# A two-way decaying scan with a binary-weight product: where ScalarE's short instructions stand, and the last batch's product turned round

## The chip, the core and the metric

The kernel runs on one core of one Trainium2 chip. Its engines work side by side and meet at semaphores: PE (TensorE, matrix products; PEld is its loading of weights), DVE (VectorE), ACT (ScalarE), POOL (GpSimd) and SP (SyncE, which here only issues DMAs). Each engine takes its instructions in the order in which the program gives them. The metric is device time in microseconds (us), lower is better.

## The reference, cut to what matters

Four batches of 1024 tokens with 1024 channels. `kv` serves as both k and v, `x` as the gate r and as the residual.

```python
tf    = sigmoid(sum(time_emb, -1))                              # one number per batch
decay = exp(-exp(w)) * (0.5 + 0.5 * tf)                         # per batch and channel
ek, ekv = exp(min(k, 30)), exp(min(k, 30)) * k
num, den = scan(ekv), scan(ek)         # forward plus backward, a = a * decay + term
num  += exp(min(u + k, 30)) * k - ekv
den  += exp(min(u + k, 30))     - ek
y     = sigmoid(x) * num / max(den, 1e-8) * (0.8 + 0.2 * tf)
alpha = mean(abs(weight), axis=1)                               # per output channel
out   = x + y @ (where(weight >= 0, 1, -1) * alpha[:, None]).T + bias
```

## The kernel before

**The blocks.** The main loop has 32 blocks `g` = 4 batches x 8 groups of 128 channels (`b, cc = divmod(g, NC)`). In a block 128 channels lie on the partitions and the 1024 tokens along the free axis, so that a scan over tokens is one DVE instruction. Everything is written out by hand under `tc.manual_schedule()`: an engine's order is the order of the statements in the loop (L456 to L541).

**DVE** does, in block g: the forward scan of num (L305), the own terms (L295), the backward scan of num (L318), the forward scan of den (L305), the newton-and-gate step of block g-1 (L357), the backward scan of den (L318), the numerator terms of block g+1 (L289), and at the head of the next block the denominator's own term (L327). A backward scan starts from a column `init`, which ACT makes from the last column of the forward scan: `act_edge` (L307), called edge_num and edge_den.

**POOL** does: the DMA that adds the own term into num (L323), the adds of x (L150, below), the floor of den of block g-1 (L333), the clamp of block g (L285), two low parts of block g-2 (L370), the product of den with the reciprocal (L350), that of num (L353) and the gated product (L360). The two low parts stand apart: one ahead of L350, one behind L353.

**ACT** does: the high parts of block g-2 (`act_hi`, L365), the scaling of product groups out of PSUM (`act_scale`, L393), Ln (`act_log`, L340), edge_num, the reciprocal as an exponential (L345), copies of turned groups to SBUF (`act_leave`, L410), the exponentials of block g+1 (L275, L281), edge_den, and in every odd block the sigmoids of the gates of blocks g+1 and g+2 (L111). A sigmoid needs another table than Ln and Exp: one table load before the sigmoids and one after (L94). From batch 1 on the first of the two sigmoids stands ahead of edge_den and the second behind it.

**The product.** gated = hi + lo, two float32r halves of a float32. A group `q` is a batch, a half of the tokens (h, 512) and 128 output channels (oc): 48 groups in batches 0 to 2, 16 in the last. `pe_product` (L375) keeps the weight's signs stationary and moves 512 tokens, 16 matmuls into one PSUM bank; the result has output channels on the partitions. So `act_scale` can scale by alpha and add the bias per partition; four transposes (`pe_turn`, L398) bring tokens back to the partitions, `act_leave` copies the group to a staging tile, and a pair of groups is stored from the SP queue. Then x is added in DRAM by a DMA that accumulates (`add_x`, L147, 128 token rows at a time, from POOL's queue). Batches 0 to 2 run nine blocks behind their scans (`lag`): two groups in most blocks, three in blocks 27, 29 and 31 (`jobs`, L420), so that all 48 are started by the end of the loop. Which block issues which add is set at L429: blocks 15 to 31 without 19 and 27, two in some, and six behind the loop.

**The tail** (L544 on) finishes block 31 and does the last batch's 16 groups. x is loaded as residual tiles (`load_residual`), up to five groups are accumulated ahead over the channel groups that are ready, the rest of block 31 is worked out (floor, den's product and the gated product on DVE; num's product on POOL), and then for each group: product, scale, four transposes, DVE's addition to the residual tile (L405), store.

Of the kernel before, what the change touches and what calls it, by code (L numbers as in the profile page):

```python
# [21 lines left out]
def kernel(  # L22
# [91 lines left out]
    def group(q):  # L114
        b, r = divmod(q, NH * NC)
        h, oc = divmod(r, NC)
        return b, h, oc


    def pair_of(t, q):  # L120
        b, h, oc = group(q)
        return t[b, h * H : (h + 1) * H, oc * P : (oc + 2) * P].rearrange(
            "(n p) c -> p n c", p=P
        )

    def hold(q, t):
        x_pairs[q] = t
        x_res[q], x_res[q + 1] = t[:, :, :P], t[:, :, P:]
# [5 lines left out]
    def load_residual(q, pool, tag):  # L134
        t = pool.tile([P, PER, 2 * P], F32, tag=tag, name=f"x_res_{q}")
        nc.sync.dma_start(out=t, in_=pair_of(x, q))
        hold(q, t)

    def store(q):
        nc.sync.dma_start(out=pair_of(out, q), in_=x_pairs[q])  # L140

    def store_one(q):
        b, h, oc = group(q)
        rows = out[b, h * H : (h + 1) * H, oc * P : (oc + 1) * P]
        nc.sync.dma_start(out=rows.rearrange("(n p) c -> p n c", p=P), in_=x_res[q])
# [34 lines left out]
    decay_ps = ps_c.tile([P, B, NC], F32, tag="decay_ps", name="decay_ps")  # L180
# [123 lines left out]
    def forward(g, t):  # L304
        nc.vector.tensor_tensor_scan(t, decay_row(g), t, 0.0, ALU.mult, ALU.add)  # L305
# [19 lines left out]
    def dve_denominator(g):  # L325
        b, cc = divmod(g, NC)
        nc.vector.scalar_tensor_tensor(  # L327
            dens[g], eus[g], top[:, b, cc : cc + 1], dens[g], ALU.min, ALU.add
        )

    def floor_den(g, engine=nc.gpsimd):
        b, cc = divmod(g, NC)
        engine.tensor_scalar(  # L333
            dens[g], dens[g], F32_MAX, floor[:, b, cc : cc + 1], ALU.min, ALU.max
        )


    def act_log(g):
        b, cc = divmod(g, NC)
        nc.scalar.activation(eus[g], dens[g], AF.Ln, scale=gain[:, b, cc : cc + 1])  # L340

    def act_reciprocal(g):
        b, cc = divmod(g, NC)
        rec = eus[g]
        nc.scalar.activation(  # L345
            rec, rec, AF.Exp, scale=-1.0, bias=ln_g[:, b, cc : cc + 1]
        )

    def den_product(g, engine=nc.gpsimd):
        engine.tensor_mul(dens[g], dens[g], eus[g])  # L350

    def pool_num_product(g):
        nc.gpsimd.tensor_mul(nums[g], nums[g], eus[g])  # L353

    def dve_newton_gate(g):
        den = dens[g]
        nc.vector.scalar_tensor_tensor(den, den, -2.0, sg_ps[g], ALU.add, ALU.mult)  # L357

    def gated_product(g, engine=nc.gpsimd):
        engine.tensor_mul(nums[g], dens[g], nums[g])  # L360
# [7 lines left out]
    def lo_part(g, h, engine=nc.gpsimd):  # L368
        t = gated[divmod(g, NC) + (h,)]
        engine.tensor_sub(  # L370
            t[:, 1, :], nums[g][:, h * H : (h + 1) * H], t[:, 0, :].bitcast(F32)
        )
# [31 lines left out]
    def dve_residual(q):  # L404
        nc.vector.tensor_add(x_res[q], x_res[q], turned[q])  # L405
# [13 lines left out]

    jobs = {g: [] for g in range(steps)}  # L420
    q = 0
    for g in range(lag, steps):
        n = 2 if g <= (B - 1) * NC + 1 or g % 2 == 1 else 3
        n = min(n, (B - 1) * NH * NC - q)
        jobs[g] = list(range(q, q + n))
        q += n
# [3 lines left out]
    for b in range(B - 1):  # L430
        for n in range(NT):
            g = (b + 1) * NC + (6 if b == B - 2 else 7 + (n >= NT // 2)) + n
            adds[min(g, steps)].append((b, n))

    with tc.manual_schedule():
# [20 lines left out]
        for g in range(steps):  # L456
            b, cc = divmod(g, NC)
            now = jobs[g]
# [20 lines left out]
            if g > 0:  # L479
                floor_den(g - 1)  # L480
                act_log(g - 1)
            pool_clamp(g)
            if g > 1:
                lo_part(g - 2, 0)
            forward(g, nums[g])
            act_edge(g, nums[g], "edge_num")
            if g > 0:
                act_reciprocal(g - 1)
                den_product(g - 1)
                pool_num_product(g - 1)  # L490
            if g > 1:
                lo_part(g - 2, 1)
# [20 lines left out]
            if b > 0 and gates:  # L513
                act_gate(gates[0])
            act_edge(g, dens[g], "edge_den")
            if leaving[1:]:
                act_leave(leaving[1])
            if g > 0:
                dve_newton_gate(g - 1)
                gated_product(g - 1)  # L520
            if len(now) > 2:
                act_scale(now[0])
            if g == 0:
                gates = (0, 1)
            for i in gates[1:] if b > 0 else gates:
                act_gate(i)
# [7 lines left out]
            if len(now) > 2:  # L534
                pe_turn(now[0])
                act_leave(now[0])
                pe_product(now[2], range(NC))
# [3 lines left out]
            leaving = now[-2:]  # L541
# [3 lines left out]
        first = (B - 1) * NH * NC  # L545
        end = B * NH * NC
        early = ps_k.tile([P, 2, H], F32, tag="kT", name="early_k")
        prods[first], prods[first + 1] = early[:, 0, :], early[:, 1, :]
        for i in range(2):
            load_residual(first + 2 * i, rows, "k_rows")  # L550
        for i in range(2):
            pe_product(first + i, range(NC - 2))

        dve_denominator(g)
        dma_own_numerator(g)
        act_hi(g - 1, 0)
        act_hi(g - 1, 1)
        for q in leaving:
            act_scale(q)
            pe_turn(q)  # L560
            act_leave(q)
        floor_den(g, nc.vector)
        lo_part(g - 1, 0)
        act_log(g)
        act_reciprocal(g)
        lo_part(g - 1, 1)
        for i in range(2, 5):
            load_residual(first + 2 * i, gate_rows, "sg_rows")
        for i in range(2, 4):
            pe_product(first + i, range(NC - 1))  # L570
        den_product(g, nc.vector)
        pool_num_product(g)
        dve_newton_gate(g)
        gated_product(g, nc.vector)
        early = ps_g.tile([P, 2, H], F32, tag="sgT", name="early_g")
        prods[first + 4], prods[first + 5] = early[:, 0, :], early[:, 1, :]
        pe_product(first + 4, range(NC - 1))
        for h in range(NH):
            act_hi(g, h)
            lo_part(g, h, nc.vector)  # L580
        for i in adds[steps]:
            add_x(*i)
        for i in range(5, NH * NC // 2):
            load_residual(first + 2 * i, eu_pool, "eu")

        rest = {first: range(NC - 2, NC), first + 1: range(NC - 2, NC)}
        for i in range(2, 5):
            rest[first + i] = range(NC - 1, NC)

        def leave(q):  # L590
            pe_turn(q)
            dve_residual(q)
            if q >= end - 2:
                store_one(q)
            elif q % 2 == 1:
                store(q - 1)

        for q in range(first, end):
            pe_product(q, rest.get(q, range(NC)))
            act_scale(q)  # L600
            if q > first:
                leave(q - 1)
        leave(end - 1)
# [30 lines left out]
```

## Time and profile before

| | us |
|---|---|
| median of 3 runs (lowest, highest) | 535.93 (534.81, 536.11) |
| the profiled execution, its own time | 535.4 |
| its span, first to last instruction | 533.5 |
| busy: DVE, POOL, PE, ACT | 455.8, 419.8, 386.3, 346.7 |
| granted TensorE clock, mean | 0.881 |
| blocks 1 to 8, each | 13.49 to 13.53 |
| blocks 9, 10, 11, 12, 13, 14 | 14.01, 13.50, 14.88, 13.50, 13.83, 13.49 |
| blocks 15 to 22 | 13.84, 13.67, 13.97, 13.79, 15.13, 13.50, 14.87, 13.50 |
| blocks 23 to 30 | 14.65, 13.77, 15.13, 13.58, 15.32, 13.79, 15.11, 14.74 |
| block 31 starts | 444.6 |

A block is counted from the start of its forward scan of num on DVE to that of the next. How to read the lines: the page gives each engine's busy time with its share of the span and its number of instructions. A row of the timeline has start, duration, engine, line of the code, operation, output <- inputs, shape; in brackets stands how long the engine had been idle and what ended that. A row of the waits says who waited for whom: us in total, how often, the longest.

### The profile page before, as it was taken

Reading aid. Unit: us, or ns where it says so; the run is one execution under the profiler, and the core shown is the slowest. Engines: PE = TensorE matmul, PEld = TensorE weight load, DVE = VectorE, ACT = ScalarE, POOL = GpSimd, SP = SyncE. Lnnn points to the kernel's source line nnn. Section 1 sums busy time; section 2 is a strip of 40 time slices with the busy share of each in tenths; the row PEclk is TensorE's granted clock in tenths of the full one; section 3 lists DMA queues with packets and bytes.
Section 4 is the critical chain, followed back from the end, with each engine's and each line's share of the span. In section 5 each row is a group of like instructions: output and inputs, shape, how many; then the busy total and the mean of one; then the engine's idle time right before and its main releaser. Section 6 shows DMA issues by size and latency. Waiting matters only on the chain.

```text
span 533.5 us, 5342 instructions
## 1 busy us (share of the span) xinstructions
PE 386.3 (72%) x1859; PEld 307.9 (58%) x1859; DVE 455.8 (85%) x295; ACT 346.7 (65%) x474; POOL 419.8 (79%) x281
## 2 busy tenths in 40 slices
PE   2444444424788777777778888778988978889995
PEld 2433333324567565655566666566866757767884
DVE  3999999999999999999998999998989899641111
ACT  4795959594758686877758585858686884431211
POOL 1179999999999899999998999999989899760000
PEclk9996555555898999999988889998899989899998
DMA  9556555544444656788867969885865978699322
GB/s 255 151 155 165 159 152 158 148 118 109 124 113 113 167 135 169 173 206 189 198 157 175 220 161 210 206 207 141 210 167 120 201 155 154 197 292 230 112 79 80
DMA packets 100579, 88.45 MB, mean 166 GB/s; under 512 B 2732, under 2 KB 89288, under 8 KB 100552
## 3 DMA queue, kind: packets, MB, share of 16 engines
q1 hardware_dynamic: 89416, 58.74, 37.8%
q0 software_dynamic: 11136, 29.36, 29.6%
q8 instruction: 15, 0.25, 0.2%
q14 instruction: 12, 0.10, 0.1%
HBM read 54.54 MB, written 29.36 MB: 157 GB/s over the span
## 4 chain that ended last, share of the span: by engine, by line
PE 30%; DVE 28%; POOL 21%; ACT 10%; issue 6%; DMA 4%; SPq 0%; POOLq 0%; ACTq 0%; DVEq 0%
PE po L381 20%; DVE den L305 5%; DVE num L318 5%; DVE num L305 5%; POOL den L350 4%; POOL num L360 4%; POOL num L353 4%; DVE den L318 4%; POOL gated L370 4%; PE turned L401 3%; DVE num L289 3%; DVE den L327 3%; POOL den L333 3%; ACT eu L340 3%; DMA sg_rows<-in_x_dram 2%
## 5 line engine op out<-in xcount | busy, mean ns | idle before, releaser
L381 PE MATMUL po<-gated,wT 128*128 128x512 f32 x960 | 261.9, 419 | 0.0
L381 PEld LDWEIGHTS po<-gated,wT 128*128 128x128 f32 x960 | 181.2, 198 | 36.8
L318 DVE TENSOR_TENSOR_SCAN den<-decay_ps,edge_den,den 128x1024 f32<-128x1024 f32 x32 | 75.0, 2344 | 8.4 <-ACT edge_den L311 8.4
L370 POOL TENSOR_TENSOR gated<-num,gated 128x512 fp32r<-128x512 f32 x62 | 80.2, 1294 | 2.4
L353 POOL TENSOR_TENSOR num<-num,eu 128x1024 f32<-128x1024 f32 x32 | 77.3, 2417 | 4.3 <-ACT eu L345 3.9
L350 POOL TENSOR_TENSOR den<-den,eu 128x1024 f32<-128x1024 f32 x31 | 73.9, 2385 | 7.4 <-ACT eu L345 5.2
L318 DVE TENSOR_TENSOR_SCAN num<-decay_ps,edge_num,num 128x1024 f32<-128x1024 f32 x32 | 75.0, 2342 | 5.1 <-ACT edge_num L311 5.1
L401 PE MATMUL turned<-ident,z 128*128 128x128 f32 x256 | 41.1, 285 | 47.9 <-ACT z L393 45.8
L263 PE MATMUL kT<-ident,k_rows 128*128 128x128 f32 x256 | 45.3, 335 | 41.5 <-issue 38.2
L365 ACT CAST gated<-num 128x512 fp32r<-128x512 f32 x64 | 36.4, 616 | 59.7 <-POOL num L360 54.8
L360 POOL TENSOR_TENSOR num<-den,num 128x1024 f32<-128x1024 f32 x31 | 74.1, 2391 | 0.5 <-DVE den L357 0.5
L269 PE MATMUL sgT<-ident,sg_rows 128*128 128x128 f32 x256 | 43.2, 324 | 42.6 <-DVE den L357 37.0
L305 DVE TENSOR_TENSOR_SCAN num<-decay_ps,num 128x1024 f32<-128x1024 f32 x32 | 72.9, 2280 | 0.0
L305 DVE TENSOR_TENSOR_SCAN den<-decay_ps,den 128x1024 f32<-128x1024 f32 x32 | 72.3, 2261 | 0.0
L393 ACT ACTIVATE z<-po,wub,out_scale 128x512 f32<-128x512 f32 x60 | 44.5, 772 | 39.3 <-PE po L381 39.3
L263 PEld LDWEIGHTS kT<-ident,k_rows 128*128 128x128 f32 x256 | 37.6, 175 | 52.6 <-issue 43.1
L401 PEld LDWEIGHTS turned<-ident,z 128*128 128x128 f32 x256 | 31.0, 144 | 63.1 <-ACT z L393 56.0
L269 PEld LDWEIGHTS sgT<-ident,sg_rows 128*128 128x128 f32 x256 | 35.0, 167 | 53.9 <-DVE den L357 27.0
L333 POOL TENSOR_SCALAR den<-den,floor 128x1024 f32<-128x1024 f32 x31 | 41.9, 1353 | 22.1 <-DVE den L327 19.6
L340 ACT ACTIVATE eu<-den,gain 128x1024 f32<-128x1024 f32 x32 | 36.8, 1151 | 20.8 <-POOL den L333 20.6
L405 DVE TENSOR_TENSOR x_res<-x_res,turned 128x512 f32<-128x512 f32 x16 | 11.0, 687 | 45.4 <-PE turned L401 45.4
L327 DVE SCALAR_TENSOR_TENSOR den<-eu,top,den 128x1024 f32<-128x1024 f32 x32 | 43.6, 1362 | 0.0
(64 smaller groups left out, 526.4 us busy)
## 6 DMA issues: line engine op xcount, KB each, us to landing
k_rows<-in_fside_BxSxS_dram SPq DMA_DIRECT2D x32, 512.0 KB, 4.8
sg_rows<-in_x_dram SPq DMA_DIRECT2D x32, 512.0 KB, 5.6
num<-euk POOLq DMA_DIRECT2D x32, 512.0 KB, 6.0
out_dram<-staged SPq DMA_DIRECT2D x24, 512.0 KB, 3.6
out_dram<-in_x_dram POOLq DMA_DIRECT2D x24, 512.0 KB, 9.9
w_rows<-in_L_ffn_weight_dram SPq DMA_DIRECT2D x8, 512.0 KB, 5.0
x_res<-in_x_dram SPq DMA_DIRECT2D x8, 512.0 KB, 7.3
out_dram<-x_res SPq DMA_DIRECT2D x7, 512.0 KB, 5.4
```

The costliest lines, as they stand in the source:

```text
L263: nc.tensor.transpose(kT[:, s * P : (s + 1) * P], k_rows[g][:, s, :], ident)
L269: nc.tensor.transpose(t[:, s * P : (s + 1) * P], sg_rows[g][:, s, :], ident)
L305: nc.vector.tensor_tensor_scan(t, decay_row(g), t, 0.0, ALU.mult, ALU.add)
L318: nc.vector.tensor_tensor_scan(back, decay_row(g), back, inits[g, which], ALU.mult, ALU.add)
L327: nc.vector.scalar_tensor_tensor(dens[g], eus[g], top[:, b, cc : cc + 1], dens[g], ALU.min, ALU.add)
L333: engine.tensor_scalar(dens[g], dens[g], F32_MAX, floor[:, b, cc : cc + 1], ALU.min, ALU.max)
L350: engine.tensor_mul(dens[g], dens[g], eus[g])
L353: nc.gpsimd.tensor_mul(nums[g], nums[g], eus[g])
L360: engine.tensor_mul(nums[g], dens[g], nums[g])
L370: engine.tensor_sub(t[:, 1, :], nums[g][:, h * H : (h + 1) * H], t[:, 0, :].bitcast(F32))
L381: nc.tensor.matmul(prods[q], wT[:, cc, oc * P : (oc + 1) * P], gated[b, cc, h][:, i, :], start=(cc == 0 and i == 0), stop=(cc == NC - 1 an ...
L401: nc.tensor.transpose(t[:, s, :], z_sb[q][:, s * P : (s + 1) * P], ident)
```

## The change

1. From batch 1 on, as in batch 0, both sigmoids stand behind edge_den.
2. In a block that has an add of x, edge_num stands ahead of Ln; else behind it, as before.
3. Two groups in every block from 9 on (`groups_of`). Two groups of batch 2 (46 and 47) are left for the tail.
4. One add of x in every block from 15 to 31, seven behind the loop.
5. Both low parts stand ahead of den's product on POOL.
6. The own numerator's DMA of block 31 is issued within the loop, ahead of the gated product of block 30.
7. The tail: block 31 is worked on in halves of 512 tokens, all on DVE and ACT (num's product and the low parts of block 30 too). The last batch's product is turned: a slice of gated (128 tokens) is stationary, 512 output channels of the weight's signs move, tokens come out on the partitions, and nothing has to be transposed. Alpha is then needed along the free axis: eight matmuls of a broadcast column with the identity spread it (`pe_spread`), ACT copies it to SBUF. The bias comes as rows by a broadcasting DMA and is added to the rows of x by DVE (`dve_add_bias`). `leave_wide` is two DVE instructions and a store of 256 KB. Six of the 16 parts (rows 0 to 2) are accumulated ahead, over seven of eight channel groups. PE's order is: group 46, turns of 44 and 45, group 47, the spread, part (0,0), turn of 46, (0,1), turn of 47, (1,0) to (2,1), then the last channel group of these six, then rows 3 to 7 whole. The bank of PSUM that held `decay_ps` is used by one of them.

```diff
-    decay_ps = ps_c.tile([P, B, NC], F32, tag="decay_ps", name="decay_ps")
+    bank = ps_c.tile([P, H], F32, tag="bank", name="bank")
+    decay_ps = bank[:, : B * NC].rearrange("p (b n) -> p b n", n=NC)
...
+    def pe_spread(column_of, bank, part):
+        for j in range(PER):
+            oc = part * PER + j
+            nc.tensor.matmul(
+                bank[:, j * P : (j + 1) * P],
+                column_of(oc).to_broadcast([P, P]), ident, start=True, stop=True,
+            )
+    def pe_wide_product(n, part, blocks):
+        h, s = divmod(n, PER)
+        for cc in blocks:
+            for i in range(2):
+                nc.tensor.matmul(
+                    wide[n, part],
+                    gated[last, cc, h][:, i, s * P : (s + 1) * P],
+                    wT[:, cc, part * H : (part + 1) * H],
+                    start=(cc == 0 and i == 0), stop=(cc == NC - 1 and i == 1),
+                )
+    def dve_add_bias(n):
+        nc.vector.tensor_add(x_rows[n], x_rows[n], bias_rows)
+    def leave_wide(n, part):
+        cols = slice(part * H, (part + 1) * H)
+        t = work.tile([P, H], F32, tag="z", name=f"wide_{n}_{part}")
+        nc.vector.tensor_mul(t, wide[n, part], alpha_rows[:, cols])
+        nc.vector.tensor_add(x_rows[n][:, cols], x_rows[n][:, cols], t)
+        nc.sync.dma_start(
+            out=out[last, n * P : (n + 1) * P, cols], in_=x_rows[n][:, cols]
+        )
...
-        n = 2 if g <= (B - 1) * NC + 1 or g % 2 == 1 else 3
+    def groups_of(g):
+        return [2 * (g - lag), 2 * (g - lag) + 1] if g >= lag else []
...
-            g = (b + 1) * NC + (6 if b == B - 2 else 7 + (n >= NT // 2)) + n
-            adds[min(g, steps)].append((b, n))
+            adds[min((b + 1) * NC + NC - 1 + n, steps)].append((b, n))
...
                 floor_den(g - 1)
-                act_log(g - 1)
             pool_clamp(g)
             if g > 1:
                 lo_part(g - 2, 0)
+                lo_part(g - 2, 1)
             forward(g, nums[g])
-            act_edge(g, nums[g], "edge_num")
+            if adds[g]:
+                act_edge(g, nums[g], "edge_num")
+            if g > 0:
+                act_log(g - 1)
+            if not adds[g]:
+                act_edge(g, nums[g], "edge_num")
             if g > 0:
                 act_reciprocal(g - 1)
                 den_product(g - 1)
-                pool_num_product(g - 1)
-            if g > 1:
-                lo_part(g - 2, 1)
+                num_product(g - 1)
...
-            if b > 0 and gates:
-                act_gate(gates[0])
             act_edge(g, dens[g], "edge_den")
             if leaving[1:]:
                 act_leave(leaving[1])
+            if g == steps - 1:
+                dma_own_numerator(g)
             if g > 0:
                 dve_newton_gate(g - 1)
                 gated_product(g - 1)
...
-            for i in gates[1:] if b > 0 else gates:
+            for i in gates:
                 act_gate(i)
...
+        for n in range(2):
+            load_x_rows(n, rows, "k_rows")
+        bias_rows = own.tile([P, C], F32, tag="euk", name="bias_rows")
+        nc.sync.dma_start(out=bias_rows, in_=bias.unsqueeze(0).to_broadcast([P, C]))
+        for n in range(2, 5):
+            load_x_rows(n, gate_rows, "sg_rows")
+        for ts in halves:
+            dve_denominator(g, ts)
+        now = groups_of(steps)
+        act_scale(leaving[0])
+        pe_product(now[0], range(NC))
+        act_scale(leaving[1])
+        for h in range(NH):
+            act_hi(g - 1, h)
+        for ts in halves:
+            floor_den(g, ts, nc.vector)
+            act_log(g, ts)
+        for ts in halves:
+            act_reciprocal(g, ts)
+        pe_turn(leaving[0])
+        act_leave(leaving[0])
+        for h in range(NH):
+            lo_part(g - 1, h, nc.vector)
+        pe_turn(leaving[1])
+        act_leave(leaving[1])
+        pe_product(now[1], range(NC))
+        act_scale(now[0])
+        act_scale(now[1])
...
+        for n in range(4):
+            dve_add_bias(n)
+        for h, ts in enumerate(halves):
+            den_product(g, ts, nc.vector)
+            num_product(g, ts, nc.vector)
+            dve_newton_gate(g, ts)
+            gated_product(g, ts, nc.vector)
+            act_hi(g, h)
+        pe_turn(now[1])
+        act_leave(now[1])
...
+        for i in waiting:
+            pe_wide_product(*i, range(NC - 1, NC))
+            leave_wide(*i)
+        for n in range(3, NT):
+            for part in range(2):
+                if n > 3:
+                    wide[n, part] = ps_o.tile([P, H], F32, tag="po", name=f"po_{n}_{part}")
+                pe_wide_product(n, part, range(NC))
+                if n > 4 and part == 0:
+                    dve_add_bias(n)
+                leave_wide(n, part)
+            if n == 3:
+                dve_add_bias(4)
```

## The prediction

> **What bounds the kernel now.** I read the page first, then the waits, then the timeline. A block g (0 to 31) here runs from the start of its forward scan of num (L305) to the next one; "+x" is x us into a block.
>
> ```profile
> span 533.5 us, 5342 instructions
> PE 386.3 (72%) x1859; PEld 307.9 (58%) x1859; DVE 455.8 (85%) x295; ACT 346.7 (65%) x474; POOL 419.8 (79%) x281
> ```
>
> DVE is fullest, but over the tail, too. In blocks 1 to 8 its scans start every 13.50 us without a gap: that is its own work, and the floor of a block. Blocks 9 to 14 take 83.2 us (six times 13.50 is 81.0), blocks 15 to 30 take 228.4 (216.0), block 31 idles 1.3. So 16 us stand above the floor. The list of waits says what DVE waits for there:
>
> ```profile
> DVE den L318 <- ACT edge_den L311: 8.4, 12, 1.6
> DVE num L318 <- ACT edge_num L311: 5.1, 5, 1.3
> ```
>
> Both backward scans wait for a one-column ScalarE instruction that stands behind something else. Block 21 (from 300.14) in the timeline shows the first kind:
>
> ```profile
> 306.74 1.11 ACT L281 ACTIVATE eu<-kT,u_g 128x1024 f32<-128x1024 f32 x1
> ...
> 307.87 1.28 ACT L111 ACT_TABLE_LOAD   x1
> 307.95 1.19 DVE L357 SCALAR_TENSOR_TENSOR den<-den,sgT 128x1024 f32<-128x1024 f32 x1
> ...
> 309.16 1.07 ACT L111 ACTIVATE sg_rows<-sg_rows 128x1024 f32<-128x1024 f32 x1
> ...
> 310.12 0.28 ACT L311 ACTIVATE edge_den<-den,edge 128x1 f32<-128x1 f32 x1
> ...
> 310.44 2.35 DVE L318 TENSOR_TENSOR_SCAN den<-decay_ps,edge_den,den 128x1024 f32<-128x1024 f32 x1 [1.29 <-ACT edge_den L311]
> ```
>
> A table load and a sigmoid (2.3 us) stand ahead of edge_den, and DVE idles 1.29. The edge_num waits are all in blocks 23, 27, 29, 30 and 31, where Ln starts 2.7 to 3.4 us in, either because POOL's floor is late behind two adds of x, or because ACT waits for a third product (1.5 us, blocks 27, 29, 31).
>
> What remains when both go? POOL, blocks 16 and 17:
>
> ```profile
> 231.93 1.05 POOL L285 TENSOR_SCALAR den<-den 128x1024 f32<-128x1024 f32 x1
> 233.06 1.28 POOL L370 TENSOR_TENSOR gated<-num,gated 128x512 fp32r<-128x512 f32 x1
> 234.41 2.40 POOL L350 TENSOR_TENSOR den<-den,eu 128x1024 f32<-128x1024 f32 x1
> ...
> 242.68 0.92 POOL L323 DMA_DIRECT2D num<-euk  x1
> 243.29 1.27 POOL L150 DMA_DIRECT2D out_dram<-in_x_dram  x1
> 244.00 1.74 POOL L333 TENSOR_SCALAR den<-den,floor 128x1024 f32<-128x1024 f32 x1
> 245.82 1.05 POOL L285 TENSOR_SCALAR den<-den 128x1024 f32<-128x1024 f32 x1
> ```
>
> No idle time is marked: from one clamp to the next POOL needs 13.89 us with one add of x (13.83 to 13.90 over ten such rounds), and some 12.5 of work without one. It is a second floor, 0.37 above DVE's.
>
> **Blocks 0 to 14.** Only the second low part (L370, 1.25) moves: it now stands ahead of den's product. From floor's start the product ends after 1.19 + 1.12 + 1.35 + 1.25 + 2.35 = 7.26 us, the floor starts at +0.27, so at +7.5; the newton step on DVE comes at +7.8. Cost 0, cover 0.3. From block 9 both sigmoids come behind edge_den (+7.9, its operand's time; exponentials end by +7.7), which removes its stall. Their four instructions (1.28 + 1.06 + 1.06 + 1.28) and the leave then end at +13.4; behind them queue hi (1.14) and the scales (1.44), so ACT is free 2.5 into the even block. With no add, Ln stays first, and edge_num ends at +3.85 where DVE wants it at +3.4: 0.45 lost in blocks 12 and 14 (block 9 has no leave, so 10 escapes). 81.0 + 0.9 = 81.9: gain 1.3.
>
> **Blocks 15 to 30.** Every block has one add (blocks with two, and 19 and 27 with none, are gone), and edge_num waits for the forward scan alone (+2.2) and for the scales (+2.5): ready by +2.8, no stall. Queued behind it are Ln, the reciprocal and, through it, POOL's den product: Ln 2.5 to 3.6, reciprocal to 4.7, while POOL needs it at +5.8. No third product, so no 1.5 us wait of a scale. Now POOL sets the pace: 13.87 a block. DVE follows: newton 7.36 after floor's start, the next block 5.68 after newton (322.82 to 328.50), so floor trails the block's start by 13.87 - 13.04 = 0.8. Block 15 starts at 216.2 - 1.3 = 214.9, its floor at 215.2; sixteen rounds later 437.1; block 31 starts at 436.3 against 444.6. Gain 8.3 up to here.
>
> One rule of the Trainium skill bears on the even blocks, where PE waits longest for the scale: "TensorE: Matmul & The Clock Gate" ("Part 1: The HAM clock gate") holds that the array falls to half clock only after an idle window of about 3.4 us. The row at 301.30 has eight products at 3.61 us instead of 2.1, granted clock 0.56, and PE had idled only 2.16 just before. By the rule the later scale (PE idle some 2.5) costs nothing; by the row kT comes 1.5 later, edge_den ends at +9.0 instead of +8.2, and newton ends at +9.3. Either way the sum is the same, with 0.3 of cover.
>
> **The tail,** from block 31's start. PE before: the last product's weights end at 526.55, +82.0; the end +88.9. After: POOL's gated product(30) ends at +13.5 (the own numerator's DMA, 0.6, now ahead of it). PE ends its last product of the block at +12.1 (newton ends +9.2, eight transposes 1.1, eight products 1.8). Then it must do 32 products of batch 2 and 256 of batch 3: 288 x 0.2231 (16 weight loads in 3.57) = 64.3; four turns 2.4 (0.59 each, where before had 17 to go); eight spreads of the scale: no row of that kind, between a turn's 0.15 and L243's 0.42 each, 1.2 to 3.4, I take 1.6 (same shape as the turn). One stall: turn 45 wants the leave of 44, which ACT does behind hi(30), two Ln and two exponentials by halves (+18.4), 2.1 after PE is ready. Sum: +12.1 + 70.4 = +82.5.
>
> DVE's chain beside it: den from +13.5 to 14.8, floors to 15.6, low parts of 30 to 17, four bias adds (1.23 each, row of DVE's L350, behind loads landing by about +22) to 22.5, eight half products (0.69) to 28, hi behind the leave of 46 to 29.7, low parts to 31. PE asks for them at +44. Cover 13. Here the skill speaks against the change: "SBUF — State Buffer" ("SBUF: two separate sides") holds that a DVE operation with two SBUF inputs and a GpSimd operation lock each other out whole. The row agrees: L327 at 457.30 takes 2.52 instead of 1.28, ending 1.07 after POOL's L360. The rule makes den wait for gated(30), 1.9 (counted), and if each of the seven adds of x (1.42 on POOL) held DVE up too, 10 more; by the rows alone none. Hidden by 13 either way. DVE's leaving (0.69 + 0.69 a part, 1.2 a row of bias) is under 4.0 per 7.1 of PE. SP: the loads of x_rows 0 to 4 and the bias go out when gates and scans are done; rows 5 to 7 and the stores stand behind the stores of 44 to 47 (+32), needed from +61.
>
> ```profile
> 518.80 3.57 PEld L381 LDWEIGHTS po<-gated,wT 128*128 128x128 f32 x16
> 522.41 0.59 PEld L401 LDWEIGHTS turned<-ident,z 128*128 128x128 f32 x4
> 522.97 3.57 PEld L381 LDWEIGHTS po<-gated,wT 128*128 128x128 f32 x16
> ```
>
> A group costs 4.17 before, 3.57 after. After the last one: before 6.95 (scale, turn, the last additions to 529.63, then 3.9 for the store); after 0.15 + 0.69 + 0.69 + 3.9 = 5.4. So +87.9: gain 1.0.
>
> Sum: 436.3 + 87.9 = 524.2 us of span, 9.3 less. The profiled execution took 535.4, 1.9 over its span: 526.1; the median of the runs, 535.93, lies 0.5 above: **526.5 us**.
>
> **Rivals.** (a) The above, 0.60; own range 523 to 530. (b) DVE stays the floor, 13.50 a block, because POOL's issue overlaps: 16 x 0.37 = 5.9 less, 520.6. Against it ten rounds at 13.87; 0.08. (c) The tail gives back: x rows and bias (2.5 MB) or the chain through ACT come later than +44, or PE falls to half clock in its stall; 3.4 us at half clock costs 1.7, a landing 5 us over the cover costs 5: 530 to 533, say 531. For it: the DMA share is 1.04 in block 31; 0.18. (d) The change does nothing that lasts: the edges' idle time turns into as much idle time before newton, which waits for POOL; a round of 14.3 and a worse tail give 535; 0.05. (e) Slower: the reciprocal is late. In even blocks ACT enters 2.5 late; if the reciprocal ends later than +5.8 POOL waits, newton with it, eight times. It cancels the gain at +5.8 + 9.3/8 = +7.0; at +7.5 it costs 13.6: 540. Against it: my count has it at +4.7; before, in blocks 27 and 29, POOL did wait 2.03 and 1.24 for it; 0.09.
>
> **The numbers.** 0.3% (1.6 us) is about what a measurement of this kernel can tell from no change. Faster is a, b and c, 0.86; same d, 0.05; slower e, 0.09. The range 521 to 532 leaves out e, d, the top of c and half of b.
>
> **What would show it.** Edge_den waits gone and edge_num under 1.5 us in all, blocks 15 to 30 at 13.8 to 13.9, POOL without idle time in them and DVE idle 0.3 before newton; block 31 from 436; products 0.223 apart to +82.5, end +88. Wrong: even blocks over 14.2 with POOL waiting for L341 (after), or PE idle behind hi(31).

## The result: 532.4 us, and a tail that grew

The changed kernel takes 532.43 us (median of 12 runs, 530.79 to 534.23), the kernel before 535.58 (12 runs beside them, 533.08 to 536.83): ratio 0.9944, 95% interval 0.9924 to 0.9964. It is faster by 3 us (0.6%) instead of the 9 forecast, and lies 0.4 above the forecast's range. The profiled execution took 531.14, 1.3 under the median.

The text ahead of the forecast puts three groups of the kernel before into blocks 27, 29 and 31; they are in blocks 26, 28 and 30. ACT's wait for the third group's scale, which is what the forecast read, falls into the block after each. Block 31 of the kernel before has one group.

The page of the changed kernel (its own line numbers: 346 is den's product, 353 the newton step, 442 and 443 the two instructions of a leaving, 428 the turned product):

```profile
span 529.4 us, 5226 instructions
PE 373.2 (71%) x1811; PEld 298.3 (56%) x1811; DVE 478.3 (90%) x328; ACT 338.5 (64%) x461; POOL 414.6 (78%) x278
```

DVE's busy share rose from 85% to 90%: the idle time ahead of its scans is gone, and the tail gave it more to do. The list of waits has, of what bound the loop before, only this left (who waited for whom, us in total, times, longest):

```profile
DVE den L353 <- POOL den L346: 3.2, 14, 0.3
...
DVE den L309 <- ACT edge_den L302: 0.9, 2, 0.5
```

Edge_den was 8.4 and is 0.9; edge_num (5.1) no longer appears among the waits; all idle time ahead of that scan is 0.3. In their place newton waits 0.2 a block for POOL. The timeline of POOL shows its pace, from clamp to clamp 13.90 (243.96 to the next at 257.86), with no idle time marked:

```profile
241.44 1.27 POOL L140 DMA_DIRECT2D out_dram<-in_x_dram  x1
242.15 1.74 POOL L326 TENSOR_SCALAR den<-den,floor 128x1024 f32<-128x1024 f32 x1
243.96 1.04 POOL L276 TENSOR_SCALAR den<-den 128x1024 f32<-128x1024 f32 x1
245.08 2.54 POOL L368 TENSOR_TENSOR gated<-num,gated 128x512 fp32r<-128x512 f32 x2
247.58 2.39 POOL L346 TENSOR_TENSOR den<-den,eu 128x1024 f32<-128x1024 f32 x1
...
257.86 1.04 POOL L276 TENSOR_SCALAR den<-den 128x1024 f32<-128x1024 f32 x1
```

| | before | forecast | after |
|---|---|---|---|
| blocks 9 to 14, sum | 83.2 | 81.9 | 81.4 |
| a block from 16 on | 13.50 to 15.32 | 13.87 | 13.89 to 13.93, but 28: 14.38, 29: 13.49, 30: 13.82 |
| block 31 starts | 444.6 | 436.3 | 436.6 |
| from there to the span's end | 88.9 | 87.9 | 92.8 |
| span | 533.5 | 524.2 | 529.4 |

Blocks 28 to 30 are one event: the granted clock was 0.76 over block 28, and 29 and 30 gave its lost time back; in the changed kernel run again all three take 13.90 or 13.91. The loop gave 8.0 of the 8.3 forecast. The tail took 3.9 back instead of giving 1.0. In it PE stands twice where nothing had been foreseen. The timeline (start, duration, engine, line; in brackets the idle time and what ended it):

```profile
482.00 0.69 DVE L442 TENSOR_TENSOR wide<-bank,alpha_rows 128x512 f32<-128x512 f32 x1 [12.54 <-PE bank L428]
482.03 0.42 PEld L428 LDWEIGHTS early_k<-wT,gated 128*128 128x128 f32 x2
482.25 0.62 PE L428 MATMUL early_k<-wT,gated 128*128 128x512 f32 x2
482.72 0.69 DVE L443 TENSOR_TENSOR x_rows<-x_rows,wide 128x512 f32<-128x512 f32 x1
483.33 0.68 DVE L442 TENSOR_TENSOR wide<-early_o,alpha_rows 128x512 f32<-128x512 f32 x1
484.05 0.69 DVE L443 TENSOR_TENSOR x_rows<-x_rows,wide 128x512 f32<-128x512 f32 x1
484.66 0.68 DVE L442 TENSOR_TENSOR wide<-early_k,alpha_rows 128x512 f32<-128x512 f32 x1
485.38 0.69 DVE L443 TENSOR_TENSOR x_rows<-x_rows,wide 128x512 f32<-128x512 f32 x1
485.40 0.30 PEld L428 LDWEIGHTS early_k<-wT,gated 128*128 128x128 f32 x2 [2.95 <-DVE wide L442]
...
491.50 3.52 PEld L428 LDWEIGHTS early_g<-wT,gated 128*128 128x128 f32 x16 [1.22 <-DVE wide L442]
...
495.07 29.26 PEld L428 LDWEIGHTS po<-wT,gated 128*128 128x128 f32 x128
```

PE finishes part (1,0) at 482.9 and may not begin part (1,1) until DVE has read (1,0), five DVE instructions later. The two parts are the two halves of one PSUM tile (early_k, 128 x 2 x 512); parts (3,0) and (3,1) share early_g in the same way. The parts with a tile of their own (bank, early_o, early_t, po), which are written and left in the same order, show no such wait. The last row is the eight parts of rows 4 to 7, without a wait.

### The profile page after: what moved, and what is told of

Same layout as the page of the kernel before. It is cut to its first block, busy times and chain, and to the rows that moved or that the text cites. A ratio compares the mean times of both kernels' runs of the same rounds, so it can differ in the third digit from the quotient of the medians.

```text
span 529.4 us, 5226 instructions
## 1 busy us (share of the span) xinstructions
PE 373.2 (71%) x1811; PEld 298.3 (56%) x1811; DVE 478.3 (90%) x328; ACT 338.5 (64%) x461; POOL 414.6 (78%) x278
## 4 chain that ended last, share of the span: by engine, by line
DVE 45%; POOL 20%; PE 14%; ACT 11%; issue 9%; DMA 1%; SPq 0%; POOLq 0%; DVEq 0%
DVE den L309 8%; DVE num L296 8%; DVE num L309 8%; DVE den L296 7%; POOL den L346 6%; PE po L428 6%; DVE den L319 4%; POOL gated L368 4%; DVE num L280 4%; DVE den L353 3%; POOL num L349 3%; POOL num L358 2%; ACT sg_rows L111 2%; DVE euk L286 2%; POOL den L276 2%
## 5 line engine op out<-in xcount | busy, mean ns | idle before, releaser
L379 PE MATMUL po<-gated,wT 128*128 128x512 f32 x768 | 209.9, 418 | 0.0
L379 PEld LDWEIGHTS po<-gated,wT 128*128 128x128 f32 x768 | 143.4, 197 | 28.4
L309 DVE TENSOR_TENSOR_SCAN den<-bank,edge_den,den 128x1024 f32<-128x1024 f32 x32 | 75.0, 2343 | 0.9 <-ACT edge_den L302 0.9
L309 DVE TENSOR_TENSOR_SCAN num<-bank,edge_num,num 128x1024 f32<-128x1024 f32 x32 | 74.9, 2339 | 0.3
L296 DVE TENSOR_TENSOR_SCAN num<-bank,num 128x1024 f32<-128x1024 f32 x32 | 72.9, 2278 | 0.0
L296 DVE TENSOR_TENSOR_SCAN den<-bank,den 128x1024 f32<-128x1024 f32 x32 | 72.3, 2259 | 0.0
L334 ACT ACTIVATE eu<-den,gain 128x1024 f32<-128x1024 f32 (+1 forms) x33 | 36.7, 1116 | 11.7 <-POOL den L326 11.0
L140 POOL DMA_DIRECT2D out_dram<-in_x_dram x24 | 28.3, 1332 | 20.1 <-DMA out_dram<-staged 20.1
L319 DVE SCALAR_TENSOR_TENSOR den<-eu,top,den 128x1024 f32<-128x1024 f32 (+1 forms) x33 | 43.8, 1329 | 0.0
L276 POOL TENSOR_SCALAR den<-den 128x1024 f32<-128x1024 f32 x32 | 33.3, 1042 | 13.1 <-DVE num L280 10.7
```

Of the source, the lines that this page charges most:

```text
L276: nc.gpsimd.tensor_scalar(dens[g], dens[g], E30, 0.0, ALU.min, ALU.max)
L309: nc.vector.tensor_tensor_scan(back, decay_row(g), back, inits[g, which], ALU.mult, ALU.add)
L319: nc.vector.scalar_tensor_tensor(dens[g][:, ts], eus[g][:, ts], top[:, b, cc : cc + 1], dens[g][:, ts], ALU.min, ALU.add,)
L379: nc.tensor.matmul(prods[q], wT[:, cc, oc * P : (oc + 1) * P], gated[b, cc, h][:, i, :], start=(cc == 0 and i == 0), stop=(cc == NC - 1 an ...
```

## The experiments

All edits are to the changed kernel unless said otherwise. "Block 31" is where it starts in the profiled execution, "tail" what follows to the span's end. A ratio is to runs of the kernel before on the same chip. Four chips were used, on which its medians were 534.22 to 534.84 us (535.58 in the result above), so that medians of versions from different chips compare only to about 1 us. "One run" has one time and no ratio.

### The changed kernel again

> The changed kernel again, beside the others on one chip. Its tail, from the start of block 31 to the end of the span, is 92.8 us in the first profile (436.6 to 529.4), against 87.9 in the forecast. Expected again: block 31 at 436 to 437, PE idle twice behind DVE after +44 (2.5 to 3.0 and 0.8 to 1.2), tail 92.5 to 93.5, time 531 to 534.

Block 31 at 436.4, tail 92.6, the same two waits (2.95 and 1.22); 531.19 us, ratio 0.9933 (0.9910 to 0.9956). As expected.

### Both products ahead of both leavings

```diff
         for i in waiting:
             pe_wide_product(*i, range(NC - 1, NC))
+        for i in waiting:
             leave_wide(*i)
```

and for row 3 `leave_wide` behind the second `pe_wide_product`.

> Order alone: the last products of all six waiting parts are issued ahead of the first leaving, and both products of row 3 ahead of its leavings. Theory W (two parts that share one tile of PSUM wait for each other: PE may not write the second while DVE has yet to read the first): both waits of PE go, the tail is 4.2 us shorter (88.4 to 89), time 4 us under the changed kernel's. Theory D (DVE's leaving of six parts, 12 instructions of 0.69, bounds PE at that place, so that the wait only moves to the banks of row 4): PE waits as long at row 4, tail within 1 of 92.8.

528.06 us, ratio 0.9871 (0.9836 to 0.9905), 3.1 under the changed kernel run again; tail 88.9, 3.7 under (4.2 expected). In the timeline PE runs through while DVE leaves the same parts at the same times:

```profile
482.08 0.69 DVE L442 TENSOR_TENSOR wide<-bank,alpha_rows 128x512 f32<-128x512 f32 x1 [12.92 <-PE bank L428]
482.11 0.87 PEld L428 LDWEIGHTS early_k<-wT,gated 128*128 128x128 f32 x4
...
483.95 7.05 PEld L428 LDWEIGHTS early_g<-wT,gated 128*128 128x128 f32 x31
...
488.72 0.68 DVE L442 TENSOR_TENSOR wide<-early_t,alpha_rows 128x512 f32<-128x512 f32 x1
```

Theory W holds: both waits are gone, and PE's wait was one of order around a shared tile. DVE, on which theory D put the blame, ends its six parts at 490.1 as before (490.2) and holds nobody up.

### The turn of group 45 behind the product of 47

```diff
+        pe_product(now[1], range(NC))
         pe_turn(leaving[1])
         act_leave(leaving[1])
-        pe_product(now[1], range(NC))
```

> Order alone: PE's product of group 47 is issued ahead of the turn of group 45. In the changed kernel PE idles 2.0 to 2.3 us ahead of that turn (at +18.6, behind ACT's Ln and exponentials). If all that follows hangs on PE, the tail is 2.2 us shorter (90.6). If ACT's chain (the scale of 47, the copy of alpha, the leave of 46) or the chain to the last high part of block 31 sets the time instead, PE waits for one of them later and the tail stays within 0.7 of 92.8.

530.65 us, ratio 0.9926 (0.9893 to 0.9958); tail 92.1, only 0.5 less. The wait at +18.6 is gone, and the wait at the shared tile comes 2.1 earlier. But then PE falls to half clock. The stretches of this run (start:end, length, busy time of PE, PEld, DVE, ACT, POOL with the number of instructions, granted clock, DMA share, GB/s):

```profile
478.00:483.00 5.00, 2.55 (x12) 1.75 (x10) 3.25 (x5) 0.00 (x0) 0.00 (x0) 1.00 1.13 205
483.00:491.00 8.00, 7.14 (x23) 5.40 (x24) 5.60 (x10) 0.00 (x0) 0.00 (x0) 0.79 1.07 289
```

In that second stretch sixteen products of early_g span 5.16 us instead of 3.83, and the two of early_t ahead of them 0.95 instead of 0.62. The wait of 2.96 before them so cost another 1.6, and 0.5 of the 2.1 is left. Neither side of the expectation: PE waits for nobody new, yet the tail keeps most of the time. The lines are of one of five runs; all five lie between 529.97 and 531.21.

### Both reorderings

> Both reorderings. If each wait is PE's own and nothing stands behind it, they add up: 6.4 us, tail 86.4, time 526. If shortening one exposes the DVE chain (low parts of block 31 at +32.9, asked for at +44), still 10 us of cover, so no loss is expected from it; if stores pile up on SP, the last store lands later than 3.2 us after the last addition.

525.09 us, ratio 0.9818 (0.9779 to 0.9857), 6.1 under the changed kernel run again (6.4 expected); tail 86.6 (86.4 expected), PE without a wait from the last gate's transposes to the end. Measured apart the two edits gave 3.7 and 0.5 of the tail, together they give 6.0: the turn's 2.1 counts once the wait that brought the half clock is gone, too.

### Three groups in blocks 26, 28 and 30 again

The old `jobs` and the three places of the loop that serve a third group come back; products 46 and 47, the turns of 44 to 46 and their copies leave the tail.

```diff
-            now = groups_of(g)
+            now = jobs[g]
...
-            leaving = now
+            leaving = now[-2:]
```

> The changed kernel with the old sharing of groups: three in blocks 26, 28 and 30, so that batch 2's products end with the loop; the tail has no product of batch 2 and one turn instead of four. Theory T (the two groups left for the tail cost there what they weigh on PE, since the tail is PE's): 32 products (7.1), three turns (1.8), the wait of 2.2 and the one scale less, tail 81.5 to 82.5; the loop pays 0.3 to 0.5 in each of blocks 27 and 29 for the late scale, block 31 at 437 to 438.5; time 522 to 525. Rival L (blocks 26 to 31 go back to 15.1 to 15.3 in every second one, as before): block 31 at 440 or later and a net gain under 7; and if DVE's chain then sets the tail, PE waits for the low parts of block 31 (at about +33) and the tail is 84 or more.

523.86 us, ratio 0.9811 (0.9783 to 0.9840): 7.3 less than the changed kernel run again, on another chip; 7.5 less by the profiled spans. Tail 82.7 (9.9 less), block 31 at 438.8 (2.4 later: blocks 27, 29 and 30 take 14.31, 15.12 and 14.77). Theory T, with block 31 0.3 later and the tail 0.2 longer than it said. What the change moved out of the loop weighs four times as much in the tail.

### The first sigmoid back ahead of edge_den

```diff
+            if b > 0 and gates:
+                act_gate(gates[0])
             act_edge(g, dens[g], "edge_den")
...
-            for i in gates:
+            for i in gates[1:] if b > 0 else gates:
```

> The changed kernel with the first of the two sigmoids back ahead of edge_den from batch 1 on. Theory S (the sigmoid alone made the 8.4 us of edge_den waits): they come back, block 31 at 443 to 445. Theory H (it made 0.3 a block where the exponentials were on time, and more only where PE was at half clock and kT late, and from block 15 on POOL's pace covers 0.4 of it): blocks 9, 11 and 13 grow by 0.3 to 0.5 each and the blocks after them lose their 0.2, odd blocks from 17 on by at most 0.3; block 31 at 437 to 439.5; time 1 to 3 us over the changed kernel's.

536.98 us, ratio 1.0052 (1.0026 to 1.0079); block 31 at 443.1, as theory S had it. Theory H is wrong. Odd blocks take 14.4 to 14.9, even ones 13.50: with edge_num ahead of Ln the reciprocal, a leave and the exponentials end at +7.2 where no transpose is late, so that edge_den comes at +9.5 (+8.95 in the kernel before). In the other odd blocks it comes at +9.8 to +10.0. The sigmoids' place is worth 6.5 us in the changed loop (5.8 by medians).

### The sigmoids alone, in the kernel before

```diff
-            if b > 0 and gates:
-                act_gate(gates[0])
             act_edge(g, dens[g], "edge_den")
...
-            for i in gates[1:] if b > 0 else gates:
+            for i in gates:
```

> The kernel before with the one edit of the sigmoids, both behind edge_den from batch 1 on. If the sum of waits is the gain: 8.4 less at edge_den, block 31 at 436 to 438, time 527 to 529. If the even blocks pay (ACT enters them 2.5 late, Ln and the reciprocal are late, POOL waits 0.9 for the reciprocal with one low part ahead, and edge_num comes after +3.4): 0.5 to 0.7 in each of ten even blocks, block 31 at 440 to 444, time 531 to 536.

534.93 us, ratio 1.0005 (0.9987 to 1.0024). Alone the same edit is worth nothing that can be measured. The waits for edge_den are gone and others stand in their place:

```profile
POOL den L350 <- ACT eu L345: 8.7, 8, 2.4
DVE num L318 <- ACT edge_num L311: 6.3, 5, 2.3
```

POOL's waits for the reciprocal were 5.2 in all before, by the page's row of L350. Of the 8.7 now, 2.6 stand in blocks 10, 12, 14 and 20, because ACT enters even blocks late; blocks 12 and 14 take 14.06 instead of 13.50. Another 4.7 stand in blocks 27, 29 and 31, where the scale of a third group is late (3.7 before); block 29 takes 16.20 instead of 15.11. Block 31 at 442.4, inside the span expected of the second case, though the even blocks were only a part of it.

### The low parts apart again

```diff
             if g > 1:
                 lo_part(g - 2, 0)
-                lo_part(g - 2, 1)
...
                 num_product(g - 1)
+            if g > 1:
+                lo_part(g - 2, 1)
```

> The changed kernel with the second low part back behind num's product on POOL. Theory P (POOL's work of 13.9 us a block is the pace, and DVE's 0.2 us ahead of newton is only how it follows): that wait goes, the blocks stay 13.88 to 13.92, block 31 within 0.4 of 436.5. Rival N (the wait for den's product holds the loop): blocks 13.65 to 13.7, block 31 at 433.

Both theories missed. One run: 543.46 us, block 31 at 445.6, 9.0 later than with the low parts together, and blocks from 15 on of 14.30 to 14.33 (26: 14.59). POOL in block 16:

```profile
233.70 1.28 POOL L368 TENSOR_TENSOR gated<-num,gated 128x512 fp32r<-128x512 f32 x1
235.52 2.41 POOL L346 TENSOR_TENSOR den<-den,eu 128x1024 f32<-128x1024 f32 x1 [0.53 <-ACT eu L341]
237.87 2.39 POOL L349 TENSOR_TENSOR num<-num,eu 128x1024 f32<-128x1024 f32 x1
240.21 1.29 POOL L368 TENSOR_TENSOR gated<-num,gated 128x512 fp32r<-128x512 f32 x1
```

The reciprocal ends at +4.8 since Ln stands behind the scales and edge_num. With one low part ahead POOL is ready at +4.4 and idles 0.5; with both, it works 1.25 in that gap. On an engine that is itself the pace, that idle time lengthens each block. DVE shows no wait for it: it takes the time at the denominator's own term, which lasts 2.08 us in block 16 instead of 1.35 and ends 1.08 after POOL's gated product. The tail is 3.5 longer than in the changed kernel run again, with half clock (granted 0.50 and 0.52) in two stretches of 3.4 us, so that its part is not put down to the edit.

### Both low parts ahead, in the kernel before

The same lines moved the other way.

> The kernel before with the one edit of the low parts, both ahead of den's product. The reciprocal there ends at +3.8, so that POOL does not wait for it in most blocks and the second low part only makes den's product late: newton waits 0 to 0.3 where POOL is late, against less waiting for the reciprocal in blocks 27, 29 and 31 (2.0, 1.2, 0.5). If the move is worth something only together with the late reciprocal: block 31 at 443.5 to 446.5. If it is worth something by itself (9 us, as the run with the low parts apart lost): block 31 at 438 or earlier.

One run: block 31 at 442.0, 532.62 us. Between the two cases, nearer the first: POOL still waits 0.8 and 0.5 for the reciprocal in blocks 27 and 29, newton waits 0.2 in seven blocks, and blocks 19 and 21 are 1.3 and 1.0 shorter than in the first profile, where PE's half clock had fallen on them. How much of the 2.6 is the edit's is left open.

### No add of x within the loop

```diff
-            for i in adds[g]:
-                add_x(*i)
```

> The changed kernel without the 17 adds of x that stand within the loop (x is left out of those rows of the output; the seven behind the loop stay). If POOL's issue of the add is what lifts a block from 13.5 to 13.9: all blocks from 15 on take 13.50 (even ones at most 13.55), POOL's round has idle time again, block 31 at 430 to 430.7. If ACT or PE holds the blocks at 13.9: little changes, block 31 over 434.

One run: blocks 13.49 to 13.58 (12 and 14: 13.7), block 31 at 430.5. The edit also takes away the adds' traffic in DRAM, but POOL's other instructions last as long as before (den's product 2.38 us, the gated product 2.40); what is new is idle time where the add stood:

```profile
268.59 1.11 POOL L326 TENSOR_SCALAR den<-den,floor 128x1024 f32<-128x1024 f32 x1 [0.65 <-DVE den L319]
```

So POOL's issue of one add lifts a block from 13.5 to 13.9, 6 us over the loop. POOL is the second floor.

### Ln ahead of edge_num in every block

```diff
-            if adds[g]:
-                act_edge(g, nums[g], "edge_num")
             if g > 0:
                 act_log(g - 1)
-            if not adds[g]:
-                act_edge(g, nums[g], "edge_num")
+            act_edge(g, nums[g], "edge_num")
```

> The changed kernel with Ln ahead of edge_num in every block, blocks with an add too. Theory A (with one add and two groups a block, Ln starts at +2.1 and edge_num ends at +3.4, when DVE wants it; POOL's pace covers the rest): at most 0.1 a block, block 31 at 436 to 437.5, so that the order of the two was worth nothing by itself in the changed loop. Theory B (the order was what removed the 5.1 us of edge_num waits): DVE waits 0.3 or more in most blocks from 16 on, block 31 at 440 or later.

One run: block 31 at 436.4, blocks 13.84 to 13.93, no edge_num wait. Theory A: once a block has one add and two groups, the order of the two is worth nothing in POOL's shadow. The time, 532.73, lies within what the changed kernel takes when run again (530.76 to 532.98), but the tail, 94.6, is 2.0 longer. 1.6 of it is half clock on PE behind the wait at the shared tile:

```profile
487.00:490.50 3.50, 3.50 (x10) 2.73 (x9) 3.18 (x5) 0.00 (x0) 0.00 (x0) 0.53 0.97 369
```

The same stretch of the changed kernel run again has the full clock and 15 matmuls instead of 10:

```profile
487.00:490.50 3.50, 3.37 (x15) 2.44 (x13) 2.91 (x6) 0.00 (x0) 0.00 (x0) 1.00 0.81 312
```

### Put together

Three groups, products first, and edge_num first in every block, those without an add (0 to 14) too:

> A version made of what the runs showed: the changed kernel with three groups in blocks 26, 28 and 30 again (tail 82.7, block 31 at 438.8), with both products ahead of both leavings where two parts share a tile (4.2 less), and with edge_num ahead of Ln in every block (blocks 12 and 14 lose their 0.2). If the parts add up: block 31 at 438.0 to 438.6, tail 78.4 to 79, time 518.5 to 520. If the two waits of PE had covered something (stores, DVE's leaving of six parts), the tail stays over 80.

522.30 us, ratio 0.9752 (0.9731 to 0.9772). The tail is 78.8 as the parts say, block 31 is at 442.2, 4 late: blocks 1 to 7 took 13.72 to 13.74 instead of 13.50, block 12 took 14.57, and blocks 27 to 30 took 14.87, 13.89, 15.14 and 14.96. The same with the order of the changed kernel, Ln first in all blocks without an add:

> Three groups in blocks 26, 28 and 30 and both products ahead of the leavings, with Ln and edge_num ordered as in the changed kernel (Ln first in blocks 9 to 14). The version that also had edge_num first missed its sum: block 31 at 442.2 instead of 438.3. If edge_num first did that (through a later reciprocal in blocks without an add): block 31 at 438.5 to 439.5 here, time 519 to 520.5. If it was the place of PE's half-clock windows, which differs from one execution to the next: block 31 anywhere from 438.5 to 442.5, the odd ones among blocks 27 to 30 at 14.3 to 15.1 as there, time 520 to 522.5.

519.53 us, ratio 0.9721 (0.9669 to 0.9774); block 31 at 439.0, tail 78.8. Of the 3.2 us by which block 31 is earlier, 1.7 are edge_num's order, though not in blocks 9 to 14: blocks 1 to 7 are back at 13.50. Block 3 in the run before (it starts at 52.48) and in this one (51.92):

```profile
61.30 0.30 ACT L302 ACTIVATE edge_den<-den,edge 128x1 f32<-128x1 f32 x1
61.64 2.35 DVE L309 TENSOR_TENSOR_SCAN den<-bank,edge_den,den 128x1024 f32<-128x1024 f32 x1
...
59.85 0.29 ACT L302 ACTIVATE edge_den<-den,edge 128x1 f32<-128x1 f32 x1
60.85 2.34 DVE L309 TENSOR_TENSOR_SCAN den<-bank,edge_den,den 128x1024 f32<-128x1024 f32 x1
```

With edge_num first, Ln starts at +2.5 instead of +1.4, and all that ACT does behind it (the reciprocal, the work on the weight, the exponentials) is later by about as much. Edge_den ends at +9.1 instead of +8.2, after DVE is ready for it, and DVE's scan starts 0.23 later in each of seven blocks. So in batch 0 the order that the changed kernel has is the right one.

The rest lies in blocks 12 and 27. PE fell to half clock in block 12 in both runs, after waits of 3.18 and 3.17 us. In the run before it lasted 6.8 us from 0.5 into the block (granted 0.51) and took in the turn (1.12 us), its eight products (3.76) and the transposes of kT (k turned for the exponentials); ACT waited 2.46 for kT, and DVE then 1.00 for edge_den, not for edge_num. Here it lasted 3.4 from 2.5 into the block (0.50), the turn took 0.66, the products 3.44, ACT waited 1.65 and DVE not at all. Block 27 took 14.30 and not 14.87: its edge_num waited 0.26 and not 0.85, with a half-clock window in block 26 of the run before and none here; it has an add, so its order is the same in both. For blocks 9 to 14 the two runs leave open what edge_num's order is worth (block 14 took 13.56 with edge_num first and 13.71 here). Last, the scale of a third group's last partner behind the reciprocal:

```diff
-            for q in leaving:
+            late = leaving[1:] if g > 0 and len(jobs[g - 1]) > 2 else []
+            for q in leaving[: len(leaving) - len(late)]:
                 act_scale(q)
...
                 act_reciprocal(g - 1)
+                for q in late:
+                    act_scale(q)
```

> The same, and in the blocks that follow three groups the scale of the last group stands behind the reciprocal instead of ahead of edge_num. If the loop pays for three groups because ACT stands at the scale of a product that PE has not done (edge_num late by 0.8 to 1.9 in blocks 27, 29 and 31): those waits go, block 31 at 436.5 to 438, tail 78.4 to 79, time 516 to 518.5. If PE itself is short in those blocks (48 products, 11 us, and 24 transposes), kT and the exponentials are late, edge_den waits appear in blocks 27 to 30, and block 31 stays at 439 or later.

516.10 us, ratio 0.9658 (0.9620 to 0.9696). Blocks 27 and 29 take 13.95 and 13.92: ACT had stood at a scale whose product PE had not done, with edge_num behind it. Block 31 at 438.1 in spite of a block 14 of 14.71 (granted clock 0.77 over it); block 30 alone is still long (14.58), with a wait of 0.44 for edge_den. The tail, 76.6, is 2 under what was expected, since block 31 itself no longer waits for edge_num (1.88 in the run above). This version beats both kernels: 16.3 us under the changed one by medians of different chips (ratios 0.9658 and 0.9944).

## Why the prediction was wrong

**The loop was right.** Forecast 436.3 for block 31, measured 436.6, 436.4, 436.7, 436.5 and 436.7 in five executions with this loop. A little of that agreement is luck: block 15 came 0.4 early, and the sixteen blocks from there took 0.7 more than forecast. POOL as second floor at 13.87 (13.90), newton's wait 0.3 (0.23), edge_den's stall gone, no stall at edge_num from 15 on: each is in the lines above, and the run without adds shows the floor to be POOL's issue. Blocks 12 and 14 lost 0.2 instead of 0.45.

**Two of its edits were worth more than their own line in it.** "Cost 0" for the second low part's new place held: newton waits 0.23 for it, inside POOL's pace. But the forecast, which had the reciprocal at +4.7 and POOL's need of it at +5.8, did not see that the move fills a wait: with only one low part ahead the loop is 9.0 longer. In the kernel before, the same move brought 2.6 at most. And the stall that the sigmoids made would have been larger in the changed order of ACT than it was before, 0.9 to 1.4 us in every odd block from 9 to 29. Alone the sigmoids' new place is worth nothing in the time, in company 5.8 (6.5 at block 31).

**The tail failed at "Sum: +12.1 + 70.4 = +82.5".** Its first half held: the turn at +18.6 (forecast +18.4), the last channel group at +44.5 (+44.1), DVE's and ACT's chains hidden with more than 10 to spare. Then the sum has 172 products at 0.2231 and nothing else. Measured, PE's last weights end at 524.33, +87.7: 4.17 in two waits for DVE at shared PSUM tiles, 0.65 because a part of sixteen takes 3.66 from start to start (the forecast divided 3.57, the length of one group's sixteen loads, which leaves out the step to the next), 0.4 from the first half. The store was 0.3 shorter. That is 4.9. That DVE's leaving "is under 4.0 per 7.1 of PE" was true and beside the point: the question was not how much DVE does but what PE may not write until DVE has read. With the order of products and leavings changed the tail measures 88.9, where the forecast had 87.9.

Of the 5.9 us between forecast and median the loop has another 0.3, and 0.8 is the step from a profiled execution to the median: I took the 0.5 of the kernel before, and it was 1.3. The cause of that stays open. Executions of the changed kernel differ by 3.4 us. Half clock behind the wait at the shared tile stands in four of the eight profiles that have this wait and is worth 1.3 to 1.6 us there; that it makes the spread was not shown.

**What the forecast didn't ask.** It weighed the third group by the 1.5 us for which a scale waits, and the two groups in the tail by 7.1 us of products, and never set the one against the other. On the chip the exchange loses 7.3 us by medians: 9.9 in the tail against 2.4 in the loop.

**The rivals.** (c), the tail gives back, has the nearest time, 531, but mostly for other causes than it named: rows and bias did come late (bias adds waited 3.0 and 1.7 us for their DMAs), within the cover, and half clock came behind a stall that (c) did not have. (b), (d) and (e) did not happen; (e)'s mechanism, POOL waiting for the reciprocal, is what the low parts prevent.

**The rules.** The lock between DVE and GpSimd showed again: the two halves of the last denominator took 3.24 us, against 1.28 for a whole one, ended 1.22 after POOL's gated product, and were hidden as forecast. Of the clock, the row was the better guide than the rule in the Trainium skill's "TensorE: Matmul & The Clock Gate" ("Part 1: The HAM clock gate"): half clock followed waits of 2.95 us, under the 3.4 of its idle window. In the changed kernel's loop that was covered (block 28, above); in the tail nothing covers it.

## What to carry to other kernels

When an order of work is turned so that PE writes two results into one PSUM tile, ask which reader must finish before the second may be written, and issue both products before either reader, or give each its own tile (the parts with a tile of their own had no wait; the two pairs were not tried so). A move on one engine that looks free should be costed in the company of the others: which gap does it fill, and which of the other edits made that gap. An order that is free in a block where another engine is the pace can cost in the blocks where it is not (0.23 in each of blocks 1 to 7). Work moved from a loop where it hides to a tail where its engine is alone costs its full length there.

## What was not expected of the hardware

Half clock on PE came in stretches of about 3.4 us behind the wait of 2.95 us at the shared tile in four of the eight profiles that have it (granted clock 0.51 to 0.53 over 3.5 us in three of them), while the same place had the full clock, 1.00, in the other four. It cost 1.3 to 1.6 us each time, 1.3 of it in one run at sixteen matmuls (5.16 instead of 3.83). An accumulating DMA of 512 KB cost POOL's queue enough (rows of 1.24 to 1.30 us) to lift a block of 13.5 us to 13.9, in each of blocks 16 to 30. The float32 spread of alpha stands in the trace as sixteen matmuls for eight instructions, 0.12 us each.
